# A spline convolution on one Trainium2 core: silu's products of two strips together on 64x32 tiles, and the first loads in another order

## The chip, the core and the metric

The kernel is one program on one core of a Trainium2 chip. The metric is the device time of one execution, in microseconds (us); less is better. The core has a matrix engine (TensorE, PE), three engines for elementwise work (VectorE or DVE, ScalarE or ACT, GpSimd or POOL), a queue that issues transfers (SyncE, SP), a memory of 128 partitions on the chip (SBUF) and banks for matmul results (PSUM). Each engine takes its instructions in the order in which they stand in the program and waits for others on semaphores.

## The reference

Four layers work on x of 8 images, 16 channels and 256 x 256 pixels, in float32. Each normalises its input by groups and adds its result to it: `x = x + layer(_gn(x), ...)`. Layer 0 is a convolution with routing, layer 2 attention over patches, layer 3 a convolution. The change is in layer 1, a 3x3 convolution in which every input value goes through silu and through eight cubic splines on a fixed grid, each with weights of its own:

```python
patches = _extract_patches(x, KSIZE, STRIDE, PAD)
grid = _grid()
bspl = _b_splines(patches, grid)
base_w = base_weight.sum(axis=2)
spl_w = (spline_weight * spline_scaler[..., None]).sum(axis=2)
out = jnp.einsum('bjhwn,ijn->bihw', jax.nn.silu(patches), base_w)
out = out + jnp.einsum('bjhwns,ijns->bihw', bspl, spl_w)
out = out + bias_weight[None, :, None, None]
```

## The kernel before

The layers follow one another in time: layer 0 up to about 4305 us of the profiled execution, layer 1 up to about 6135, then layers 2 and 3. `layer1` walks over 8 images of 16 strips, 128 strips in all, of 16 rows each. Even and odd rows are kept apart, so a strip is 8 pairs of rows.

*Bases.* `features` brings a strip in with a broadcast load of 1 MB (`xr`, L994): 16 channels, two rows of a pair and four grid offsets make the 128 partitions. In two halves of four pairs it makes two kinds of bases. ACT takes distances (L1012, L1015), DVE clips them twice (L1023, `a` and `e`), ACT squares both (L1029), DVE multiplies to cubes (L1032), POOL subtracts (L1041, the first kind, called total here), and DVE masks that into the second kind (L1044). At an image's ends DVE sets the rows outside (L1049). Three sets of bases (`ring`) stand in turn. DVE's L1023, L1044 and L1049 and POOL's L1041 are marked "shared" for the planner below.

*Silu.* `silus` loads a strip's raw rows twice, one row apart by two (`rs`, L1071), and the rows to be added to (`res`). ACT makes the silu (L1082) in four buffers `sring`, two for a strip.

*Products.* `conv_strip` sums a strip in one PSUM buffer `ps`, of which there are two. PE is used as four column tiles of 128 rows x 32 columns, one for each group of 32 output lanes: two output rows of 16 channels. Spline products are 12 groups of four matmuls: q = 0, 1 (the pair of rows and the one below it), two kinds, three columns dx. For the last output lanes q = 1 needs the first pair of the next strip's bases. Three groups of four matmuls with the silu weights `wm` follow. A float32 matmul shows as two records in the trace. All matmuls are recorded under L1106. Then DVE adds bias and `res` (`y`, L1143, two instructions), takes statistics (L1155), and SP stores the strip (L1158).

*Weights.* `prepare` loads spline weights `sw`, scalers `sc` and silu weights `main` (L933) into the places of bases that aren't in use yet. DVE multiplies the first two (L937), PE sums over the 9 inputs (L945 for splines, L970 for silu), DVE finishes `tw` (L954 to L966), ACT copies `wm` (L982).

*Order.* Nobody writes the order of the instructions by hand. Each step is given to `_Order` with its engine, a planned duration, what it reads and writes, and for a load a lag until its data is there. `_Order.run` plays the queues of all engines forward with these costs, up to four strips ahead, and of the steps that can start takes that with the earliest due time: the strip's number times `period`, less the planned length of what follows it. It adds 0.25 us when PE changes its `mode`. What stands in each engine's queue is the order in which it took the steps. `ahead` puts in other work: layer 2's weights are loaded at strip 2, the statistics of an image taken at its end (L1177).

*After it.* Layer 2 begins in `attend`: DVE normalises a patch into `t` (L1456), POOL adds embeddings (L1460), PE multiplies (L1466). `t` is taken from the pool `mid`.

Of the kernel before, what the change touches and what calls it, by code (L numbers as in the profile page):

```python
# [9 lines left out]
F32 = mybir.dt.float32  # L10
# [6 lines left out]
B, C, H, W = 8, 16, 256, 256  # L17
P = 128
# [13 lines left out]
def _consts():  # L32

    p = np.arange(P)
    hi, lo = p // 16, p % 16

    fold = np.stack([h * 16 + lo[:, None] == np.arange(32)[None, :] for h in range(2)], 1)
    unfold = np.zeros((4, 2, C, 2, 4, P), np.float32)
    for h in range(2):
        for k in range(4):  # L40
            unfold[k, h, :, h, k] = np.arange(C)[:, None] == lo[None, :]


    sel = np.stack([16 * g + 8 * h + hi[:, None] == np.arange(32)[None, :] for g in range(2) for h in range(2)], 1)
    spread = np.zeros((4, 2, 2, 8, 2, 2, 8, C), np.float32)
    for g in range(2):
        for h in range(2):
            for b in range(8):
                spread[:, g, h, b, g, h, b] = 1.0

    diff = np.zeros((B, C, C, B), np.float32)
    for i in range(C):
        for a in range(B - 1):
            diff[a, i, i, a] = 1.0
            diff[B - 1, i, i, a] = -1.0
        diff[:, i, i, B - 1] = 1.0 / B
    parts = {

        "pair": 0.5 * (p[:, None] // 2 == p[None, :] // 2),
        "diff": diff.reshape(P, P),  # L60

        "fold": fold.reshape(P, 2 * 32),
        "unfold": unfold.reshape(P, 8 * P),

        "sel": sel.reshape(P, 4 * 32),

        "spread": spread.reshape(P, 4 * P),
        "ident": np.eye(P),

        "group": (lo[:, None] // 2 == lo[None, :] // 2) / 16.0,  # L70

        "same_lo": lo[:, None] == lo[None, :],
        "ones": np.ones((P, P)),
        "mean": np.full((P, P), 1.0 / P),

        "same_c4": lo[:, None] == p[None, :] % 64 // 4,

        "hi8": hi[:, None] == np.arange(8)[None, :],
        "row0": p[:, None] == np.arange(16)[None, :],

        "middle": -(p[:, None] % 4 - 1.5),

        "pad": _padding(),

        "keep": np.stack([p >= 16, p < 112, p >= 64, p < 64], 1),

        "ident3": _ident3(),
    }
# [41 lines left out]
def _layout(w0, bw, sw, sc, bias, wq, bq, wk, bk, wv, bv, w3):  # L130
# [14 lines left out]
    sw = np.concatenate([sw, sw])  # L145
    sc = np.broadcast_to(sc.transpose(1, 2, 3, 0).reshape(1, C, 1, 81 * C), (2, C, 4, 81 * C)).reshape(P, 81 * C)
    bt = bw.transpose(1, 2, 3, 0).reshape(C, 9, 3, 3, C)
    main = np.zeros((8, C, 9, 3, 4, 2, C), np.float32)
    for ro in range(8):
        for dh in range(3):  # L150

            ri = ro + dh - 1 + (1 if ro < 6 else -1)
            main[ri, :, :, :, ro // 2, ro % 2] = bt[:, :, dh]
    main = main.reshape(P, 9 * 3 * P)
    b1 = np.tile(bias, 8).reshape(P, 1)

    qk = np.concatenate([wq.T, wk.T], 1).reshape(2, P, 512).transpose(1, 0, 2)
# [148 lines left out]
class _Net:  # L306
# [544 lines left out]
    def layer1(self, bc, bc4, images=range(B), strips=range(16)):  # L851
# [7 lines left out]
        with ExitStack() as st:  # L859
            one = st.enter_context(tc.tile_pool(name="l1_one", bufs=1))  # L860

            tw = one.tile([P, 2, 2, 3, 2, C], F32, name="tw")
            wm = one.tile([P, 3, 4, 2 * C], F32, name="wm")
            sbuf = st.enter_context(tc.tile_pool(name="l1_sb", bufs=1))
            psum = st.enter_context(tc.tile_pool(name="l1_ps", bufs=1, space=PSUM))
            b1 = one.tile([P, 1], F32, name="b1")
# [34 lines left out]

            places = dict(xr=3, d=3, a=3, e=3, res=4, rs=4, y=2)
            banks = dict(sq=3, ps=2)
            order = _Order({**places, **banks}, 13.3)

            def buf(kind, shape):
                n = {**places, **banks}[kind]
                pool = psum if kind in banks else sbuf
                return _Buf(kind, lambda: pool.tile(shape, F32, name=f"{kind}1", tag=kind, bufs=n))

            held = {}

            def edges(i, op):
                def pads():
# [9 lines left out]
            def prepare(op):  # L924

                at1, at2 = (ring[i].rearrange("p k m w -> p (k m w)") for i in (1, 2))
                sw, sc, main = at2[:, :2592], at2[:, 2592:3888], at1[:, :3456]
                ws = one.tile([P, 2, 3, 3, C], F32, name="ws")
                wf = ws.rearrange("p k h w o -> p (k h w o)")
                ps = buf("sq", [P, 1024])  # L930
                edges(0, op)
                for name, t in (("sw", sw), ("sc", sc), ("main", main), ("b1", b1)):
                    op("SP", 0.5, lambda name=name, t=t: nc.sync.dma_start(out=t, in_=self.d[name]), [], [(name,)], lag=16.0 if name == "main" else 10.0)  # L933

                def scaled():
                    for k in range(2):
# [31 lines left out]
                def sums_main():  # L968
                    for m in range(9):
                        nc.tensor.matmul(  # L970
                            ps()[:, 512:896],
                            self.k["ident"],
                            main[:, m * 384 : m * 384 + 384],
                            start=m == 0,
                            stop=m == 8,
                        )
# [1 line left out]
                op("DVE", 2.9, scaled, [("sw",), ("sc",)], [("sw",)], mode="shared")  # L978
                op("PE", 6.0, sums, [("sw",)], [(ps, 0), ("place", 2)])
                op("DVE", 3.5, finish, [(ps, 0)], [("tw",)], mode="shared")  # L980
                op("PE", 7.0, sums_main, [("main",)], [(ps, 1), ("place", 1)])
                op("ACT", 0.5, lambda: nc.scalar.copy(wm.rearrange("p d n m -> p (d n m)"), ps()[:, 512:896]), [(ps, 1)], [("wm",)])  # L982
                for i in (1, 2):
                    edges(i, op)

            def features(b, j, op):
# [12 lines left out]
                        .to_broadcast([2 * C, 4, pairs * W]),  # L999
                    )  # L1000

                op("SP", 0.5, fetch, [], [(xr, 0)], lag=6.0 if i else 13.0)
                for p in range(0, pairs, 4):
                    n = min(4, pairs - p)
                    us = 0.2 + 0.8 * n / 4
# [56 lines left out]

            def silus(b, j, op):

                i = b * 16 + j
                res = held[i] = buf("res", [P, 2, W])
                raw = [buf("rs", [P, 2, W]) for _ in range(2)]
                for r, to in ((1, res), (0, raw[0]), (2, raw[1])):

                    def fetch(r=r, to=to):  # L1070
                        nc.sync.dma_start(  # L1071
                            out=to().rearrange("p k w -> p (k w)"),
                            in_=self.x1[j, b, :, r : r + 8].rearrange("c r k w -> r c (k w)"),
                        )

                    op("SP", 0.5, fetch, [], [(to, 0)], lag=4.0 if i else 16.0)
                for n in range(2):
                    s = sring[i % 2 * 2 + n]
                    key = ("s", i % 2, n)
# [17 lines left out]

            def conv_strip(b, j, op):

                i = b * 16 + j  # L1100
                cur, res = ring[i % 3], held.pop(i)
                ps = buf("ps", [P, 2, W])

                def mm(n, k, lhs, rhs, start=False, stop=False):
                    out = ps()[32 * n : 32 * n + 32]
                    nc.tensor.matmul(  # L1106
                        out if k is None else out[:, k], lhs, rhs, start=start, stop=stop, skip_group_check=True
                    )

                for q in range(2):  # L1110
                    for kind in range(2):
                        for dx in range(3):

                            def products(q=q, kind=kind, dx=dx):
                                lhs = tw[:, kind, q, dx].rearrange("p r o -> p (r o)")
                                cols = slice(dx, dx + W)
                                both = cur[:, kind, 0:8].rearrange("p (k m) w -> p k m w", k=2)
                                for n in range(4):
                                    if n + q < 4:
                                        mm(n, None, lhs, both[:, :, n + q, cols], start=not (q or kind or dx))  # L1120
                                    else:
                                        mm(n, 0, lhs, cur[:, kind, 4, cols])
                                        last = cur[:, kind, 8] if j == 15 else ring[(i + 1) % 3][:, kind, 0]
                                        mm(n, 1, lhs, last[:, cols])
# [327 lines left out]

    def attend(self, mid, psum, b, c, pt, res, emb, wqk, wv, bqk, bv, bc, stats):
        nc = self.nc
        t = mid.tile([P, 2, 8, 32], F32, name="t")
        nc.vector.tensor_scalar(  # L1456
            t, pt[:, :, c], bc[:, 0, b, c : c + 1], bc[:, 1, b, c : c + 1], ALU.subtract, ALU.mult
        )
# [242 lines left out]
```

## Time and profile before

| what | us |
|---|---|
| median of 3 runs | 7646.63 |
| lowest and highest run | 7644.09, 7649.12 |
| the profiled execution | 7643.24 |
| its span, first to last instruction | 7641.5 |
| first load of layer 1, issued | 4305.97 |
| first product of layer 1, start | 4368.76 |
| last silu product of layer 1, start of the block | 6129.87 |
| first product of layer 2, start | 6140.35 |

The profile is one execution on the hardware. Its times are positions from the span's start. A line of a group or of a timeline names the code line (L1106), the engine, the operation and the data it wrote and read; xN is a number of records, and a bracket gives the idle time of the engine just before and what ended it. PE stands for matmuls and PEld for the loads of weights that go with them. PEclk is the share of full speed that TensorE's clock was granted.

### The profile page before, as it was taken

The numbers are of one execution on the slowest core, as the hardware profiler recorded it, in microseconds if no ns is written. First come the engines' busy times: TensorE is split into PE (matmuls) and PEld (weight loads), VectorE is DVE, ScalarE is ACT, GpSimd is POOL, SyncE is SP. The second block draws the span as 40 slices with busy tenths as digits, with TensorE's granted clock in tenths as the row PEclk, the third lists the DMA queues.
The fourth block names the chain that finished last, engine by engine and source line by source line (L and its number), as shares of the span: only waits on it lengthen the run. The fifth ranks groups of instructions, "written<-read, shape, count | busy, mean of one in ns | idle before, by whom it ended". The sixth has DMA issues, their size and how long they took to land.

```text
span 7641.5 us, 105946 instructions
## 1 busy us (share of the span) xinstructions
PE 6889.0 (90%) x43144; PEld 3276.6 (43%) x43144; DVE 5415.1 (71%) x6462; ACT 2691.9 (35%) x3835; POOL 3248.8 (43%) x1884
## 2 busy tenths in 40 slices
PE   4888888999898999998998499999999999999999
PEld 1333333333333333333333254554545566666634
DVE  5768888887888888888888688888888833333322
ACT  1222222222222222222222277777777712111200
POOL 0545555555555555555555444444444411111100
PEclk9999999999999999999999699999999999999999
DMA  6222222222222222222221344444445533333276
GB/s 243 67 65 76 77 77 77 77 77 77 77 77 77 77 77 77 77 77 76 77 76 50 105 153 156 153 152 152 154 151 161 159 114 97 86 85 97 68 214 189
DMA packets 451065, 813.01 MB, mean 106 GB/s; under 512 B 57490, under 2 KB 299282, under 8 KB 415250
## 3 DMA queue, kind: packets, MB, share of 16 engines
q1 hardware_dynamic: 380946, 738.85, 33.6%
q10 hardware_dynamic: 69632, 67.39, 3.0%
q8 instruction: 340, 5.57, 0.3%
q14 instruction: 147, 1.20, 0.1%
HBM read 595.63 MB, written 211.03 MB: 106 GB/s over the span
## 4 chain that ended last, share of the span: by engine, by line
PE 51%; POOL 21%; DVE 16%; issue 4%; ACT 3%; DMA 3%; SPq 0%; POOLq 0%; DVEq 0%; ACTq 0%
PE ps L1106 13%; POOL dd L765 11%; POOL s L765 8%; PE cv L545 8%; PE pqk L1466 6%; DVE dd L756 4%; PE p3s L1577 4%; PE cv L549 4%; PE pl L654 3%; PE po L1493 3%; PE pv L1473 3%; PE psc L1481 3%; PE fb L622 3%; DMA xr<-x1p 2%; POOL s L810 2%
## 5 line engine op out<-in xcount | busy, mean ns | idle before, releaser
L765 POOL TENSOR_TENSOR dd<-dd 128x1024 f32<-128x1024 f32 x512 | 1206.2, 2356 | 1594.9 <-DVE dd L756 1575.0
L1106 PE MATMUL ps<-bases,tw 128*32 128x512 f32 (+1 forms) x13824 | 1377.8, 550 | 109.6 <-DVE bases L1049 92.0
L756 DVE SCALAR_TENSOR_TENSOR dd<-rb,v 128x1024 f32<-128x1024 f32 (+1 forms) x1024 | 1075.2, 1082 | 206.7 <-PE rb L745 196.8
L554 ACT COPY v<-cv 128x1024 f32<-128x1024 f32 x512 | 518.2, 1012 | 1909.2 <-PE cv L549 1909.2
L1041 POOL TENSOR_TENSOR bases<-e,a 128x1024 f32<-128x1024 f32 (+1 forms) x264 | 744.9, 2823 | 1044.5 <-DVE e L1032 922.0
L545 PE MATMUL cv<-kt,w 128*128 128x512 f32 x2048 | 1090.9, 658 | 38.0 <-DVE dd L756 26.5
L1106 PEld LDWEIGHTS ps<-bases,tw 128*32 128x32 f32 x13824 | 732.4, 109 | 764.9 <-issue 458.3
L644 DVE TENSOR_TENSOR pr<-v,fb 128x2048 f32<-128x2048 f32 (+1 forms) x512 | 1019.5, 2014 | 24.9 <-PE pl L654 20.0
L745 PE MATMUL rb<-rs,ct_fold 32*128 32x512 f32 x3584 | 796.5, 658 | 8.3 <-ACT rs L727 2.7
L765 POOL TENSOR_TENSOR s<-s,dd 128x512 f32<-128x512 f32 x512 | 652.2, 1274 | 29.9
L545 PEld LDWEIGHTS cv<-kt,w 128*128 128x128 f32 x2048 | 366.1, 199 | 598.4 <-issue 389.7
L549 PE MATMUL cv<-kt,w 64*128 64x512 f32 x2048 | 590.9, 654 | 0.0
L654 PE MATMUL pl<-pr,ct_fold 128*32 128x512 f32 x3584 | 525.9, 610 | 61.0 <-DVE pr L644 60.3
L1460 POOL TENSOR_TENSOR t<-t,emb 128x512 f32<-128x512 f32 x128 | 162.1, 1266 | 961.9 <-DVE t L1456 950.8
L622 PEld LDWEIGHTS fb<-f,ct_fold 128*128 128x128 f32 x3072 | 376.7, 195 | 340.7 <-issue 296.7
L622 PE MATMUL fb<-f,ct_fold 128*128 128x128 f32 x3072 | 436.3, 290 | 90.7 <-DVE f L608 88.4
L1466 PE MATMUL pqk<-w_qk,t 128*128 128x512 f32 x1024 | 484.4, 596 | 7.6 <-POOL t L1460 7.6
L765 POOL TENSOR_TENSOR s<-v,dd 128x512 f32<-128x512 f32 x256 | 328.9, 1285 | 319.4 <-DVE dd L756 319.2
L1477 ACT ACTIVATE vt<-pv,w_b2v 128x128 f32<-128x128 f32 x512 | 146.0, 367 | 841.2 <-PE pv L1473 810.8
L1497 DVE TENSOR_TENSOR y<-po,res 128x512 f32<-128x512 f32 x128 | 88.5, 691 | 487.6 <-PE po L1493 487.6
L745 PEld LDWEIGHTS rb<-rs,ct_fold 32*128 32x128 f32 x3584 | 241.2, 188 | 380.7 <-DVE dd L756 211.7
L1032 DVE TENSOR_TENSOR e<-e,sq 128x1024 f32<-128x1024 f32 (+1 forms) x264 | 314.5, 1191 | 95.4 <-ACT sq L1029 95.4
(254 smaller groups left out, 8995.6 us busy)
## 6 DMA issues: line engine op xcount, KB each, us to landing
kt<-d SPq DMA_DIRECT2D x256, 516.0 KB
xr<-x1p SPq DMA_DIRECT2D x120, 1024.0 KB
rs<-x SPq DMA_DIRECT2D x256, 256.0 KB
d<-dn ACTq DMA_DIRECT2D x64, 516.0 KB
xs<-in_x_dram SPq DMA_DIRECT2D x16, 2048.0 KB
xs<-in_x_dram SPq DMA_DIRECT2D x64, 512.0 KB
res<-in_x_dram SPq DMA_DIRECT2D x64, 512.0 KB
x<-s SPq DMA_DIRECT2D x128, 256.0 KB
```

Source lines behind the costliest of these rows:

```text
L545: nc.tensor.matmul(ps()[:, n], w[:, 0, j, :], t[:, a : a + 2, 0:W], start=True, stop=False)
L549: nc.tensor.matmul(ps()[:, n], w[at, 1, j, :], t[at, a : a + 2, 2 - n : 2 - n + W], start=False, stop=True)
L554: nc.scalar.copy(v[h]()[:, 4 * g : 4 * g + 4, j * W : j * W + W], ps().rearrange("p n (a w) -> p (n a) w", w=W),)
L622: nc.tensor.matmul(fb()[:, k * P : k * P + P], unfold[:, h, k, :], f()[:, 3], start=True, stop=True)
L644: nc.vector.tensor_tensor(pr()[:, :n], v[h]()[:, 4 * g : 4 * g + n], p().unsqueeze(1).to_broadcast([P, n, 512]), ALU.mult,)
L654: nc.tensor.matmul(pl()[at : at + 32], sel[:, g, h, :], pr()[:, t, :], start=h == 0 and g == 0, stop=h == 1 and (g == 1 or t == 3),)
L745: nc.tensor.matmul(r()[:, n], spread[at, g, h, :], rs()[at], start=True, stop=True)
L756: nc.vector.scalar_tensor_tensor(dd()[:, :n], r()[:, :n], 1.0 / B, v[h]()[:, a : a + n], ALU.subtract, ALU.mult)
L765: op("POOL", us, lambda: nc.gpsimd.tensor_tensor(out[0](), a[0](), b[0](), ALU.add), a[1] + b[1], out[1])
L1041: nc.gpsimd.tensor_tensor(v, rows(part(e)), rows(part(a)), ALU.subtract)
L1106: nc.tensor.matmul(out if k is None else out[:, k], lhs, rhs, start=start, stop=stop, skip_group_check=True)
L1466: nc.tensor.matmul(ps, t[:, n, k * P : (k + 1) * P], wqk[:, n, :], start=n == 0, stop=n == 1)
```

## The change

Silu's weights: `main` was laid out for a matmul over eight input rows (128 partitions), with a different shift for each of the four groups of output rows. It is now laid out for four input rows (64 partitions), which holds for every group, twice over the partitions. It has 864 columns where it had 3456, and its sums and `wm` are as much narrower. DVE copies `wm`, where ACT did.

Silu's products: they are taken at the start of an odd strip's products, for that strip and the even one before it. A matmul now uses a tile of 64 rows x 32 columns; for each column group one matmul of the even and one of the odd strip stand on the two halves of the rows, and write two PSUM buffers. There are three groups of eight for a pair of strips, where each strip had three groups of four. The even strip is evicted after them. The odd strip's 12 groups of spline products come after them, and then its eviction.

Odd strips' raw rows: the two halves of the partitions are exchanged, so each of the two loads becomes two, of 64 partitions. `keep`, the mask of a row outside an image, follows that.

Ahead of the products: strip 0's `xr` is asked for before the weights, and the planned durations and lags of the first loads are set anew. Layer 2's weights are loaded at strip 6 in place of 2. The planner's `period` goes from 13.3 to 12.4, and the new silu group has the mode `r64`. In layer 2 `t` gets a pool of its own, allocated first.

```diff
-    main = np.zeros((8, C, 9, 3, 4, 2, C), np.float32)
-    for ro in range(8):
+    main = np.zeros((4, C, 9, 3, 2, C), np.float32)
+    for ro in range(2):
         for dh in range(3):
-
-            ri = ro + dh - 1 + (1 if ro < 6 else -1)
-            main[ri, :, :, :, ro // 2, ro % 2] = bt[:, :, dh]
-    main = main.reshape(P, 9 * 3 * P)
+            main[ro + dh, :, :, :, ro] = bt[:, :, dh]
+    main = np.tile(main.reshape(64, 9 * 96), (2, 1))
...
-            wm = one.tile([P, 3, 4, 2 * C], F32, name="wm")
+            wm = one.tile([P, 3, 2 * C], F32, name="wm")
...
-            order = _Order({**places, **banks}, 13.3)
+            order = _Order({**places, **banks}, 12.4)
...
-                sw, sc, main = at2[:, :2592], at2[:, 2592:3888], at1[:, :3456]
+                sw, sc, main = at2[:, :2592], at2[:, 2592:3888], at1[:, :864]
...
+                first = dict(sw=3.5, sc=1.8, main=1.2, b1=0.5)
                 for name, t in (("sw", sw), ("sc", sc), ("main", main), ("b1", b1)):
-                    op("SP", 0.5, lambda name=name, t=t: nc.sync.dma_start(out=t, in_=self.d[name]), [], [(name,)], lag=16.0 if name == "main" else 10.0)
+                    op("SP", first[name], lambda name=name, t=t: nc.sync.dma_start(out=t, in_=self.d[name]), [], [(name,)], lag=3.0)
...
-                            ps()[:, 512:896],
+                            ps()[:, 512:608],
                             self.k["ident"],
-                            main[:, m * 384 : m * 384 + 384],
+                            main[:, m * 96 : m * 96 + 96],
...
-                op("PE", 7.0, sums_main, [("main",)], [(ps, 1), ("place", 1)])
-                op("ACT", 0.5, lambda: nc.scalar.copy(wm.rearrange("p d n m -> p (d n m)"), ps()[:, 512:896]), [(ps, 1)], [("wm",)])
+                op("PE", 3.0, sums_main, [("main",)], [(ps, 1), ("place", 1)])
+                def finish_main():
+                    nc.vector.tensor_copy(wm.rearrange("p d m -> p (d m)"), ps()[:, 512:608])
+                op("DVE", 0.2, finish_main, [(ps, 1)], [("wm",)], mode="shared")
...
-                op("SP", 0.5, fetch, [], [(xr, 0)], lag=6.0 if i else 13.0)
+                op("SP", 0.5 if i > 2 else 2.8, fetch, [], [(xr, 0)], lag=6.0 if i else 8.0)
+                if not i:
+                    prepare(op)
...
-                        nc.sync.dma_start(
-                            out=to().rearrange("p k w -> p (k w)"),
-                            in_=self.x1[j, b, :, r : r + 8].rearrange("c r k w -> r c (k w)"),
-                        )
-                    op("SP", 0.5, fetch, [], [(to, 0)], lag=4.0 if i else 16.0)
+                        swap = i % 2 and r != 1
+                        for at, row, n in ((0, r + 4, 4), (64, r, 4)) if swap else ((0, r, 8),):
+                            nc.sync.dma_start(
+                                out=to()[at : at + 16 * n].rearrange("p k w -> p (k w)"),
+                                in_=self.x1[j, b, :, row : row + n].rearrange("c r k w -> r c (k w)"),
+                            )
+                    op("SP", 0.5 if i else 0.7, fetch, [], [(to, 0)], lag=4.0)
...
-                ps = buf("ps", [P, 2, W])
+                ps = open_ps[i] = buf("ps", [P, 2, W])
...
+                if i % 2:
+                    both = [(open_ps.pop(k), k) for k in (i - 1, i)]
+                    keys = [("s", k, n) for k in range(2) for n in range(2)]
+                    for dx in range(3):
+                        def silus(dx=dx):
+                            for n in range(4):
+                                for p, k in both:
+                                    half = n // 2 ^ k % 2
+                                    at = slice(64 * half, 64 * half + 64)
+                                    src = sring[k % 2 * 2 + n % 2]
+                                    mm(n, None, wm[at, dx], src[at, :, dx : dx + W], bool(k % 2 and not dx), dx == 2 and not k % 2, p)
+                        op("PE", 0.9, silus, [("wm",), *keys], [(p, 0) for p, _ in both], mode="r64")
+                    evict(b, j - 1, both[0][0], op)
...
-                for dx in range(3):
-                    def last(dx=dx):
-                        for n in range(4):
-                            src = sring[i % 2 * 2 + n // 3]
-                            mm(n, None, wm[:, dx, n], src[:, :, dx : dx + W], stop=dx == 2)
-                    op("PE", 0.86, last, [("wm",), ("s", i % 2, 0), ("s", i % 2, 1)], [(ps, 0)])
+                if i % 2:
+                    evict(b, j, ps, op)
+            def evict(b, j, ps, op):
+                res = held.pop(b * 16 + j)
                 y = buf("y", [P, 16, 2, 16])
...
-                if n == 2:
+                if n == 6:
                     for name, t in self.w2.items():
...
-                if not n:
-                    prepare(op)
                 if n < len(todo):
                     features(*todo[n], op)
...
+            self.tpool = st.enter_context(tc.tile_pool(name="l2_t", bufs=2))
...
-        t = mid.tile([P, 2, 8, 32], F32, name="t")
+        t = self.tpool.tile([P, 2, 8, 32], F32, name="t")
```

More of the change, by code (lines that the diff above doesn't have):

```diff
@@ L83, in _consts @@
         "pad": _padding(),
-        "keep": np.stack([p >= 16, p < 112, p >= 64, p < 64], 1),
+        "keep": np.stack([p >= 16, (p < 48) | (p >= 64), p >= 64, p < 64], 1),
         "ident3": _ident3(),
@@ L909, in buf @@
                 return _Buf(kind, lambda: pool.tile(shape, F32, name=f"{kind}1", tag=kind, bufs=n))
-            held = {}
+            held, open_ps = {}, {}
             def edges(i, op):
@@ L1100, in conv_strip, with mm @@
                 i = b * 16 + j
-                cur, res = ring[i % 3], held.pop(i)
-                ps = buf("ps", [P, 2, W])
-                def mm(n, k, lhs, rhs, start=False, stop=False):
+                cur = ring[i % 3]
+                ps = open_ps[i] = buf("ps", [P, 2, W])
+                def mm(n, k, lhs, rhs, start=False, stop=False, ps=ps):
                     out = ps()[32 * n : 32 * n + 32]
@@ L1117, in products @@
                                 both = cur[:, kind, 0:8].rearrange("p (k m) w -> p k m w", k=2)
+                                start = not (q or kind or dx or i % 2)
+                                stop = bool(i % 2 and q and kind and dx == 2)
                                 for n in range(4):
                                     if n + q < 4:
-                                        mm(n, None, lhs, both[:, :, n + q, cols], start=not (q or kind or dx))
+                                        mm(n, None, lhs, both[:, :, n + q, cols], start, stop)
                                     else:
-                                        mm(n, 0, lhs, cur[:, kind, 4, cols])
+                                        mm(n, 0, lhs, cur[:, kind, 4, cols], stop=stop)
                                         last = cur[:, kind, 8] if j == 15 else ring[(i + 1) % 3][:, kind, 0]
-                                        mm(n, 1, lhs, last[:, cols])
+                                        mm(n, 1, lhs, last[:, cols], stop=stop)
                             name = "vm"[kind]
```

## The prediction

> **What bounds the kernel now.** I read the shares of busy time first, then the costly groups, then layer 1 alone by stretches of time.
>
> ```profile
> PE 6889.0 (90%) x43144; PEld 3276.6 (43%) x43144; DVE 5415.1 (71%) x6462; ACT 2691.9 (35%) x3835; POOL 3248.8 (43%) x1884
> ...
> L1106 PE MATMUL ps<-bases,tw 128*32 128x512 f32 (+1 forms) x13824 | 1377.8, 550 | 109.6 <-DVE bases L1049 92.0
> ```
>
> ```profile
> 4368.70:6132.80 1764.10, 1677.94 (x16902) 885.59 (x16902) 1474.48 (x1749) 1262.77 (x1293) 734.57 (x260) 0.98 0.48 153
> ```
>
> Columns of the second: stretch, length, then busy time of PE, PEld, DVE, ACT, POOL, clock, DMA share, GB/s. Layer 1's products take 1764 us, PE is busy in 95% of it, and its idle time before the products is 110 us. So PE sets the pace within an image. DVE is the next engine, at 84%. The steady state shows in PE's timeline:
>
> ```profile
> 4706.59 2.79 PE L1106 MATMUL ps<-silu,wm 128*32 128x512 f32 x24
> 4709.16 10.55 PE L1106 MATMUL ps<-bases,tw 128*32 128x512 f32 x108
> 4719.47 2.82 PE L1106 MATMUL ps<-silu,wm 128*32 128x512 f32 x24
> ```
>
> From one silu block to the next is 12.88 us. A strip has 24 steps of four concurrent records for products and 6 for silu: 12.88/30 = 0.4295 us a step. A pair of strips takes 25.77 us. At an image's edge PE stops:
>
> ```profile
> 4589.94 10.54 PE L1106 MATMUL ps<-bases,tw 128*32 128x512 f32 x87 [9.65 <-DVE bases L1049]
> ```
>
> ```profile
> 4583.00:4593.00 10.00, 3.06 (x16) 0.90 (x20) 9.96 (x12) 4.39 (x5) 3.23 (x1) 0.51 0.63 183
> ```
>
> It waits 9.65 us for DVE, and its clock is halved into the restart. Per image before: 13 × 12.88 + 13.6 + 14.8 (two waits of about 1 and 2 us for DVE) + about 25 at the edge = 221, and 8 × 221 is the 1764 within 4. Ahead of the products:
>
> ```profile
> 4305.97 0.34 SPq L933 DMA_DIRECT2D bases<-in_main_dram  x1
> ...
> 4335.44 1.28 ACT L1082 ACT_TABLE_LOAD   x1 [29.76 <-DMA w_b2v<-in_b2v_dram]
> ...
> 4368.76 3.76 PE L1106 MATMUL ps<-bases,tw 128*32 128x512 f32 x20 [33.74 <-DVE bases L1049]
> ```
>
> ACT's first instruction is a silu whose rows are loaded late; everything behind it waits, and the first product starts 62.8 us after the first load. After the last product:
>
> ```profile
> 6138.18 1.00 DVE L1456 TENSOR_SCALAR t<-pt,g2a_bc 128x512 f32<-128x512 f32 x2 [3.03 <-issue]
> ```
>
> **What the Trainium skill says.** "TensorEngine Tiling (Array Packing)", Available Configurations, lists 64x32 as 8 independent tiles; Key Properties says that changing the mode drains TensorE. No 64x32 stands in this trace. Two row tiles do (64x128 in layer 0), concurrently; a change of mode costs 0.09 to 0.11 us there (2000.33 to 2007.3 us, the starts of L549 and L654 against their usual step). "TensorE: Matmul & The Clock Gate", Part 1, puts the clock at half after an idle window of about 3.4 us. The trace agrees so far: half clock after the 10 us gap (0.51 above), none after gaps of 2 us. "SBUF — State Buffer", Who interferes with whom, says that DVE and GpSimd lock one port pair for a whole instruction, and that issue order decides who waits. The trace agrees: L1041 on POOL takes 2.36 us alone and 3.27 when DVE's L1044 of 4710.15 started ahead of it.
>
> **The change, part by part.**
>
> *Silu on 64x32 tiles.* Per pair, 2 × 3 groups of four 128x32 matmuls (12 steps) become 3 groups of eight 64x32 (as many records, 6 steps). If eight tiles run in the time of four, PE saves 6 × 0.4295 = 2.58 us and pays two changes of mode, 0.22: 23.4 us of PE work a pair for 25.77. If eight cost like two fours, nothing is saved and 0.22 is lost. Each load of weights in the trace follows the last by 0.04 us, so eight take 0.32 of the 0.43 us step; I take full concurrency.
>
> *What the order makes of it.* PE's queue becomes: even strip's 12 groups, both silus, DVE evicts even; odd's 12 groups, DVE evicts odd; next even strip. Products with q = 1 of the even strip need row 0 of the strip after it. In the built order DVE makes those only behind the odd eviction, which itself waits for odd's last product. So a circle closes over each pair. I walk it with the trace's start-to-start times: DVE eviction 0.40, L1044 1.20, bn_stats 0.61, L1023 0.60, L1032 1.13; 0.17 from L1032's end to POOL, POOL 2.36, 0.03 on to PE or DVE. The rows are of this kind:
>
> ```profile
> 4714.91 0.68 DVE L1023 TENSOR_SCALAR a<-d 128x1024 f32<-128x1024 f32 x1
> 4715.51 0.69 DVE L1023 TENSOR_SCALAR e<-d 128x1024 f32<-128x1024 f32 x1
> ...
> 4716.71 1.21 DVE L1032 TENSOR_TENSOR a<-a,sq 128x1024 f32<-128x1024 f32 x1
> 4717.84 1.21 DVE L1032 TENSOR_TENSOR e<-e,sq 128x1024 f32<-128x1024 f32 x1
> ```
>
> From the end of odd's last product: 0.19 to the eviction; two of it, one L1044, bn_stats, three L1023 and one L1032 until POOL's first total starts, 5.79. Two more L1032 run beside that total and end 2.27 after its operand did; so the second total is ready 0.09 us before the first (2.36) is over, and POOL goes straight on. DVE's L1044, woken by the first total, comes 0.03 after its end and finds the port taken. Case A: two totals 4.60, L1044 1.28, 0.03: sum 11.9 until PE may start the last six steps of q = 1. Then 2.15 + 0.11 + 2.67 (six silu steps and their drain) + 0.11 + 10.34 (odd's 24 steps) = 15.4. The pair takes 27.27 us, of which PE is idle 3.3, in two pieces of 2.4 and 0.9; neither is long enough for the clock to fall. That is 1.5 us more than before in the steady stretch. What comes back is the edge: in the walk odd's 24 steps of an image's last strip keep PE running while DVE makes the next image's first bases, so an edge costs 3 us instead of 12 and leaves the clock alone. An image is 7 × 27.27 + 30.3 = 221.2, the same as before. Eight make 1770; I add 17 for the first two pairs (5) and for irregular places that a walk of the kernel before missed as well (some 12): 1787, or +23.
>
> *Odd strips' raw rows in swapped halves.* 128 more DMAs on SP's queue, 0.57 us to issue each, spread over 1764 us; SP is idle most of it and the transfer share is 0.48. Zero, covered by raw buffers two strips deep; without the cover half a microsecond a strip, 64 × 0.57 = 36.
>
> *Prologue.* The big broadcast goes first, then sw, sc; main is a quarter (432 KB for 1728), sums_main 96 wide for 384 (it took 5.97). ACT no longer starts with a silu. Walk: xr, sw and sc are some 3 MB, at the 410 GB/s of 4310 to 4320 us 7.5 us and 2 to land, so sc is there 9.6 after the first issue; L937 2.93; sums 7.23 behind it, 20; the weights' chain L954 to L966 took 5.5 (4353.59 to 4359.09), 26; beside it DVE and POOL make the first bases; L1044 and L1049 at the end, 29.7. Against 62.8: −33, and −25 to −38 if the loads land a few microseconds off. w2's loads, moved four strips later, leave SP's queue there; nobody needs them before layer 2.
>
> *wm copied by DVE instead of ACT, period 12.4, other lags.* 0.2 us once; the rest shows only in the order, which I walked.
>
> *t in its own pool.* DVE's 3.03 us wait ahead of layer 2 was for the last store, whose buffer t lay over. −3; zero if the loads issued at 6138.28 are then the late ones.
>
> Sum for A: −33 − 3 + 23 = −13. The profiled execution took 7643.24 (span 7641.5), 3.4 under the median 7646.63; A is 7630 against it and 7633 against the median. A measurement of this kernel tells about 0.2% (15.3 us) from no change.
>
> **The rivals.**
>
> B: DVE's L1044 gets the port between the two totals. It lacks 0.1 us: if a square on ACT or a cube is later by that, POOL's second total isn't ready. Then q = 1 runs on without its second wait; the walk gives 26.33 a pair, 216 an image, 1728 + 19 = 1747: −17. Sum −53: 7594. For it: the small margin. Against it: at 4575 us two totals stand back to back in the same pattern.
>
> C, slower: eight 64x32 matmuls don't fit a step. Place: the silu block, on the circle, so every 0.1 us of each step costs 6 × 0.1 × 64 = 38 us. It eats A's gain from 0.03 us a step (−13 + 13) and is slower by over 0.2% from 0.075. At 0.58 us a step (weight loads or PSUM in the way) it gives 7633 + 58 = 7691, with two fours 7633 + 165 = 7798. For it: the shape is nowhere in this trace, and the loads fill three quarters of a step. The skill's Gotcha 1 on that tiling page forbids two row tiles one PSUM bank at a time; the diff gives the halves different banks. Half clocks on each of 64 gaps would cost as much (1.8 each, 113).
>
> D: PE alone sets the pace, 23.4 a pair: 64 × 23.4 + 40 = 1538, −226 and −36: 7385. Against it: the circle stands in the built order. That the change does not do what it says is excluded by that order for the tiles; for the prologue it is the upper end of −25.
>
> **How the numbers follow.** A 0.45, B 0.25, C 0.25, D 0.05. Forecast: A's 7633; A's own range is 7615 to 7655 (prologue ±5 to 8, irregular places ±12). The range goes from under B to the middle price of C, 7585 to 7691; it leaves out D, C's upper half and a little of B. Faster by over 0.2% (under 7631): all of B and D, 0.13 of A: 0.43. Slower (over 7662): 0.23 of C and 0.05 of A: 0.28. Within: 0.29.
>
> **What would show it.** Silu blocks 26.3 (B) or 27.3 (A) apart for 2 × 12.88; a silu block's 48 records in 2.6 us (over 3.2: C); PE waiting about 2.4 us for POOL L1049 (the total's new line) and 0.9 for DVE once a pair; no 10 us wait at edges; the first product 30 us after the first load. A DVE that evicts odd strips without holding up the next bases would make all of A wrong.

## The result, and the profile after

| | before | after | foreseen |
|---|---|---|---|
| median of four runs | 7645.36 | 7689.09 | 7633 |
| ratio, 95% interval | | 1.0058, 1.0042 to 1.0074 | |
| span of the profiled execution | 7641.5 | 7693.0 | |
| start to the first load of layer 1 | 4306.0 | 4311.2 | 0 |
| first load to first product | 62.8 | 30.7 | −33 |
| first to last product of layer 1 | 1764.0 | 1850.5 | +23 |
| last product to the first of layer 2 | 7.6 | 4.4 | −3 |
| from there to the end | 1501.1 | 1496.2 | 0 |

The change made the kernel slower, by 44 us or 0.58%, where the forecast was no difference to speak of. The time lies at the upper end of the stated range. Three terms of the sum came as foreseen; the products of layer 1 cost 86.5 us more, not 23. The first and last rows (+5.3 and −4.9) are in code that the change leaves alone, but for t's pool. In the later kernels the first falls between 4303.8 and 4312.0 and the last between 1496 and 1500, so I take them as scatter between executions. The profiled execution, 7694.78 us, was the longest of the four.

The page after, first the shares of busy time and the group of the products, then the stretch of layer 1's products with the same columns as before:

```profile
PE 6831.9 (89%) x43144; PEld 3012.3 (39%) x43144; DVE 5508.7 (72%) x6463; ACT 2693.8 (35%) x3834; POOL 3119.0 (41%) x1884
...
L1119 PE MATMUL ps<-bases,tw 128*32 128x512 f32 (+1 forms) x13824 | 1444.0, 560 | 223.1 <-POOL bases L1049 181.7
```

```profile
4341.90:6192.40 1850.50, 1624.09 (x16902) 619.80 (x16902) 1574.10 (x1758) 1271.43 (x1300) 611.63 (x262) 0.97 0.50 147
```

PE has 54 us less to do in layer 1 (1624 for 1678), yet the stretch is longer: PE is busy in 88% of it where it was in 95%. Its idle time before products doubled to 223 us, and what ends it is now mostly POOL's total (L1049) instead of DVE's edge rows. PE no longer sets the pace.

PE's timeline over one pair in the middle of an image, as foreseen for case A:

```profile
4651.11 2.81 PE L1119 MATMUL ps<-silu,wm 64*32 64x512 f32 x48
4653.85 16.73 PE L1119 MATMUL ps<-bases,tw 128*32 128x512 f32 x164
4672.64 2.78 PE L1119 MATMUL ps<-bases,tw 128*32 128x256 f32 x30 [2.07 <-POOL bases L1049]
4676.06 2.35 PE L1119 MATMUL ps<-bases,tw 128*32 128x256 f32 x22 [0.64 <-DVE bases L1052]
4678.34 1.95 PE L1119 MATMUL ps<-silu,wm 64*32 64x512 f32 x32
```

From silu block to silu block is 27.23 us; the walk said 27.27. The block's 48 records are over 2.74 us after its start, changes of mode included: eight 64x32 tiles do run in the time of four. The two waits of the prediction are there, 2.07 and 0.64 us. But of the 63 distances between pairs only 15 look like this. A pair later in an image:

```profile
5194.02 2.81 PE L1119 MATMUL ps<-silu,wm 64*32 64x512 f32 x48
5196.75 6.21 PE L1119 MATMUL ps<-bases,tw 128*32 128x512 f32 x56
5203.45 4.94 PE L1119 MATMUL ps<-bases,tw 128*32 128x256 f32 x52 [0.48 <-POOL bases L1049]
5211.37 6.21 PE L1119 MATMUL ps<-bases,tw 128*32 128x512 f32 x56 [2.98 <-POOL bases L1049]
5218.77 2.78 PE L1119 MATMUL ps<-bases,tw 128*32 128x256 f32 x30 [1.20 <-POOL bases L1049]
5222.19 2.35 PE L1119 MATMUL ps<-bases,tw 128*32 128x256 f32 x22 [0.63 <-DVE bases L1052]
5224.47 1.95 PE L1119 MATMUL ps<-silu,wm 64*32 64x512 f32 x32
```

It takes 30.45 us, with two more waits for POOL, 0.48 and 2.98 us. The median of the 63 is 28.6. POOL is only the last link. ACT's timeline in the same stretch, and what SP issued ahead of it:

```profile
5195.12 1.24 ACT L1020 ACTIVATE d<-xr,bd,sd 128x1024 f32<-128x1024 f32 x1 [6.44 <-DMA xr<-x1p]
...
5225.79 1.24 ACT L1020 ACTIVATE d<-xr,bd,sd 128x1024 f32<-128x1024 f32 x1 [6.66 <-DMA xr<-x1p]
```

```profile
5205.69 2.39 SPq L1083 DMA_DIRECT2D rs<-x  x4
5210.73 0.62 SPq L1185 DMA_DIRECT2D x<-y  x1
5211.40 0.58 SPq L1083 DMA_DIRECT2D res<-x  x1
5212.66 12.44 SPq L1000 DMA_DIRECT2D xr<-x1p  x2
```

The strip's broadcast load xr is issued at 5212.66, when its buffer comes free, and ACT gets it at 5225.79, 13.1 us later; ACT has waited 6.66 us, and DVE, POOL and PE stand behind ACT. (The 12.44 us are those of two loads; the second waits for its buffer.) Ahead of xr on SP's queue are the four half loads of raw rows that the change made out of two. Over layer 1, ACT waits 210 us for xr; before it was 69.

At both ends the profile after reads as the prediction had it: the first product 30.7 us after the first load, and no wait ahead of `t`, against the 3.03 us of before.

```profile
4341.92 3.64 PE L1119 MATMUL ps<-bases,tw 128*32 128x512 f32 x16 [10.77 <-DVE bases L1057]
...
6194.70 0.94 DVE L1482 TENSOR_SCALAR t<-pt,g2a_bc 128x512 f32<-128x512 f32 x2
```

### The profile page after: what moved, and what is told of

Its sections match the earlier page's. It is cut to its first block, busy times and chain, and to the rows that moved or that the text cites. A ratio compares the mean times of both kernels' runs of the same rounds, so it can differ in the third digit from the quotient of the medians.

```text
span 7693.0 us, 106047 instructions
## 1 busy us (share of the span) xinstructions
PE 6831.9 (89%) x43144; PEld 3012.3 (39%) x43144; DVE 5508.7 (72%) x6463; ACT 2693.8 (35%) x3834; POOL 3119.0 (41%) x1884
## 3 DMA queue, kind: packets, MB, share of 16 engines
q1 hardware_dynamic: 380946, 737.52, 34.2%
## 4 chain that ended last, share of the span: by engine, by line
PE 46%; POOL 23%; DVE 19%; DMA 6%; issue 4%; ACT 2%; SPq 0%; POOLq 0%; DVEq 0%; ACTq 0%
POOL dd L764 11%; PE cv L544 8%; POOL s L764 8%; PE ps L1119 8%; PE pqk L1492 6%; DMA xr<-x1p 4%; PE p3s L1603 4%; DVE dd L755 4%; PE cv L548 4%; PE pl L653 3%; PE po L1519 3%; POOL bases L1049 3%; PE pv L1499 3%; PE psc L1507 3%; PE fb L621 3%
## 5 line engine op out<-in xcount | busy, mean ns | idle before, releaser
L1119 PE MATMUL ps<-bases,tw 128*32 128x512 f32 (+1 forms) x13824 | 1444.0, 560 | 223.1 <-POOL bases L1049 181.7
L544 PE MATMUL cv<-kt,w 128*128 128x512 f32 x2048 | 1094.8, 660 | 39.3 <-DVE dd L755 26.5
L1049 POOL TENSOR_TENSOR bases<-e,a 128x1024 f32<-128x1024 f32 (+1 forms) x264 | 616.4, 2345 | 1246.2 <-DVE e L1040 1180.4
L1119 PEld LDWEIGHTS ps<-bases,tw 128*32 128x32 f32 x13824 | 567.2, 111 | 1120.4 <-issue 537.3
L1052 DVE SCALAR_TENSOR_TENSOR bases<-xr,xm,bases 128x1024 f32<-128x1024 f32 (+1 forms) x264 | 455.1, 1726 | 95.2 <-POOL bases L1049 95.1
L1040 DVE TENSOR_TENSOR a<-a,sq 128x1024 f32<-128x1024 f32 (+1 forms) x264 | 315.0, 1193 | 111.2 <-ACT sq L1037 111.0
```

Source lines behind the costliest of these rows:

```text
L544: nc.tensor.matmul(ps()[:, n], w[:, 0, j, :], t[:, a : a + 2, 0:W], start=True, stop=False)
L1049: nc.gpsimd.tensor_tensor(v, rows(part(e)), rows(part(a)), ALU.subtract)
L1119: nc.tensor.matmul(out if k is None else out[:, k], lhs, rhs, start=start, stop=stop, skip_group_check=True)
```

## The experiments

The traces leave three theories. Theory 1: the circle of the prediction is right, 27.2 us a pair, and on top of it odd strips' xr lands late, behind a bunch of row loads. Theory 2: the order on the engines alone stretches the pairs. Theory 3: the half loads of 64 partitions are slow themselves. All times are medians; each was run beside the kernel before, which stayed at 7642.7 to 7643.4. Brackets give the ratio to it and its 95% interval. A pair is timed from the start of one silu block to the next, 63 times in a run.

**Order of the first loads alone (e1).** In the kernel before, with the new planned times and lags of the first loads and layer 2's weights at strip 6:

```diff
-                op("SP", 0.5, fetch, [], [(xr, 0)], lag=6.0 if i else 13.0)
+                op("SP", 0.5 if i > 2 else 2.8, fetch, [], [(xr, 0)], lag=6.0 if i else 8.0)
+                if not i:
+                    prepare(op)
...
-                if not n:
-                    prepare(op)
```

> The kernel before with the change's order of first loads alone: xr of strip 0 ahead of the weights, the new planned times and lags, layer 2's weights at strip 6; silu products and weights stay as they were. Theory 1 (the prologue is worth what the changed kernel's trace shows, a first product 32 us earlier, and is lost again in the pairs): first product 20 to 33 us earlier than before, less than the whole because main keeps its 1728 KB; steady strips stay at 12.88; about 7618 us. Rival (the reordering disturbs the strips that follow): no gain, 7640 to 7660.

7617 us (0.996, 0.9945 to 0.9975). The first product starts 38.1 us after the first load (62.8 before, 30.7 with the quarter-sized main), and the products take 1766.9 us for 1764.0. So the gain of the prologue is real and stands by itself; the changed kernel has it and loses it later.

**One raw load a strip (e2).** The changed kernel, both silus from the rows of the first; the rows of the second load are left out:

```diff
-                raw = [buf("rs", [P, 2, W]) for _ in range(2)]
-                for r, to in ((1, res), (0, raw[0]), (2, raw[1])):
+                raw = [buf("rs", [P, 2, W])] * 2
+                for r, to in ((1, res), (0, raw[0])):
```

> The changed kernel with one raw load a strip in place of two: both silus read the rows of the first (it leaves out the shifted rows of the second, and the order of the compute instructions stays). 512 KB of 4 MB a pair and 3 of 13 transfers go. Theory 1 (pairs stretch from 27.2 to 28.5-30.6 us because the odd strip's xr, issued right behind a bunch of raw rows, lands 8 to 13 us after issue in place of 5): ACT's wait for xr falls from 210 to under 80 us, most pairs are 27.2, about 7640 us. Theory 2 (the pairs stretch by the order on DVE, POOL and ACT alone): 7689, within 8 us.

7661 us (1.0022, 1.0015 to 1.0029): 28 of the 49 us that theory 1 wanted, and outside theory 2. ACT still waits 191 us, over twice what I expected. With half of the raw bytes gone xr still lands 10.1 us after issue in the median. Bytes in a bunch are not the whole of it.

**Odd rows whole (e3).** The changed kernel without the exchange of halves, so odd strips' silu products take other rows:

```diff
-                        swap = i % 2 and r != 1
+                        swap = False
```

> The changed kernel with odd strips' raw rows in one transfer of 128 partitions in place of two of 64 (the halves are not exchanged, so the odd strips' silu products take other rows); as many bytes, 128 transfers fewer. Theory 1 (bytes in a bunch): within 10 us of 7689. Theory 3 (transfers of 64 partitions are themselves slow, or 128 more issues hold SP up): ACT's wait for xr falls by more than half, about 7640 us.

7631 us (0.9984, 0.9976 to 0.9993). Theory 3's figure, not theory 1's: as many bytes as in the changed kernel, but 58 us less. 38 of 63 pairs take 27.2 to 27.3, ACT waits 97 us for xr, and the products take 1787.4 us, which is the 1787 of the prediction's case A. The pair after the longer one shown above takes 27.24 us here, for 30.64 in the changed kernel:

```profile
5184.59 2.81 PE L1119 MATMUL ps<-silu,wm 64*32 64x512 f32 x48
5187.33 16.63 PE L1119 MATMUL ps<-bases,tw 128*32 128x512 f32 x164
5206.12 2.78 PE L1119 MATMUL ps<-bases,tw 128*32 128x256 f32 x30 [2.17 <-POOL bases L1049]
5209.55 2.35 PE L1119 MATMUL ps<-bases,tw 128*32 128x256 f32 x22 [0.65 <-DVE bases L1052]
5211.83 1.05 PE L1119 MATMUL ps<-silu,wm 64*32 64x512 f32 x6
```

**Four xr buffers (e4).** The changed kernel; d has two buffers and the ninth pair is loaded by itself, to make room:

```diff
-            places = dict(xr=3, d=3, a=3, e=3, res=4, rs=4, y=2)
+            places = dict(x9=1, xr=4, d=2, a=3, e=3, res=4, rs=4, y=2)
```

> The changed kernel with four xr buffers in place of three; to make room, d has two buffers for three and the ninth pair of an image's last strip is loaded by itself. A load can be issued a strip earlier. Theory 1: the wait of ACT for xr goes nearly to zero, pairs are 27.2 to 27.3 throughout (28.5 at the second of an image), layer 1's products take about 1790 us for 1850, 7630 us. Theory 2: 7689; if two d buffers hinder ACT, more.

7629 us (0.998, 0.9972 to 0.9989), products 1787.8 us. ACT never waits for xr, though the half loads are still there. So the way by which they hurt is xr alone: given a strip's lead, they cost nothing that shows. Theory 2 is out.

**POOL made to let DVE go first (e5).** e4, with a copy of one column on POOL ahead of a strip's second total:

```diff
+                        if p == 4:
+                            nc.gpsimd.tensor_copy(look, t[:, 1, 0, 1:2])
                         nc.gpsimd.tensor_tensor(v, rows(part(e)), rows(part(a)), ALU.subtract)
```

> e4 (four xr buffers) with one more instruction on POOL ahead of the second total of a strip: a copy of one column (128x1) that DVE's masking of the first half has written. POOL must then let DVE's masking go first, which is rival B of the prediction made to happen. Theory 1 (in the changed kernel POOL's second total takes the port and DVE's masking waits a whole total for it): pairs go from 27.2 to 26.3 (second of an image 27.6 for 28.5), less some 0.1 for the copy; layer 1's products 30 us shorter than in e4, about 7600 us. Rival (who goes first doesn't matter, the sum of the two engines' work does): within 8 us of e4's 7629.

7609 us (0.9955, 0.994 to 0.997), 20 less than e4, for an expected 30. DVE's masking in the changed kernel, then POOL's two totals of that moment, then both at the same place in e5:

```profile
4672.62 3.38 DVE L1052 SCALAR_TENSOR_TENSOR bases<-xr,xm,bases 128x1024 f32<-128x1024 f32 x1 [0.31 <-POOL bases L1049]
```

```profile
4670.22 4.70 POOL L1049 TENSOR_TENSOR bases<-e,a 128x1024 f32<-128x1024 f32 x2 [5.92 <-DVE e L1040]
```

```profile
4672.80 1.29 DVE L1059 SCALAR_TENSOR_TENSOR bases<-xr,xm,bases 128x1024 f32<-128x1024 f32 x1 [0.29 <-POOL bases L1056]
```

```profile
4670.39 2.37 POOL L1056 TENSOR_TENSOR bases<-e,a 128x1024 f32<-128x1024 f32 x1 [5.19 <-DVE e L1045]
4674.15 0.58 POOL L1055 COPY look<-bases 128x1 f32<-128x1 f32 x1 [1.39 <-DVE bases L1059]
```

In the changed kernel POOL runs its two totals back to back and DVE's instruction takes 3.38 us. In e5 POOL waits, DVE's takes 1.29, and pairs go from 27.2 to 26.4 (48 of 63 between 26.3 and 26.5); the walk of rival B said 26.33. More than the missing 10 us went at images' edges, where a pair now takes 34.6 to 37.1 us for 30.2 to 33.5 in e4: the seven edges take 34 us more, the other 56 pairs 56 less. Why the edges grow the runs don't show.

**Odd eviction later (e6).** The changed kernel; an odd strip's eviction is handed to the planner with the next strip's work:

```diff
                 if i % 2:
-                    evict(b, j, ps, op)
+                    waiting.append((b, j, ps))
+                if waiting and (not i % 2 or j == 15):
+                    evict(*waiting.pop(), op)
```

> The changed kernel with the eviction of an odd strip given to the planner with the following strip's work, 12.4 us later in due time (in an image's last strip as before); transfers as in the changed kernel. Theory 1 (the pair's length is the circle over DVE: bases for the next strip stand behind the odd eviction, which waits for the odd products): the circle is broken, pairs go to 24.3 by my walk with the trace's durations where transfers allow; those that wait for xr stay longer; between 7480 and 7570 us. Rival (DVE's and POOL's sum of work or PE sets the pair's length): within 20 us of 7689.

7547 us (0.987, 0.9854 to 0.9887), 142 less than the changed kernel. 40 of 63 pairs run from 24.3 to 26.3 us, held up by xr (ACT waits 213 us for it).

**Late eviction and four xr buffers (e7).**

> e6 with e4's four xr buffers (d two, ninth pair by itself). Theory 1: both causes gone, pairs of 24.3 nearly throughout (walk: 1626 us from first to last product, plus some 15), 7629 - 149 = 7480, with 7470 to 7510 as bounds. Rival (with shorter pairs the transfers can't keep up, 4 MB in 24.3 us): 7520 to 7560, ACT waiting for xr or silu waiting for rows.

With e4's buffers added: 7475 us (0.9779, 0.9764 to 0.9793), products 1629.7 us. 40 of 63 pairs lie between 24.2 and 24.5. One of them:

```profile
4904.77 2.81 PE L1123 MATMUL ps<-silu,wm 64*32 64x512 f32 x48
4907.51 21.59 PE L1123 MATMUL ps<-bases,tw 128*32 128x512 f32 x216
4929.03 1.05 PE L1123 MATMUL ps<-silu,wm 64*32 64x512 f32 x6
```

In these 24.26 us no wait is long enough for the timeline to show it, and PE is busy for 24.12. Against e4, with the same buffers and pairs of 27.2, only the moment at which the planner gets the odd evictions is new. So the circle did set the pair's length. With the circle gone PE is nearly always busy, except in the first pairs and at the edges of images, which still take 26.6 to 34.2 us.

**Halves exchanged by ACT (e8).** The changed kernel with rows loaded whole, and silu of odd strips in two instructions that write to the other 64 partitions:

> The changed kernel with odd strips' raw rows loaded whole, and their halves exchanged by ACT: silu of an odd strip in two instructions of 64 partitions that write to the other half, each as long as one of 128 (1.5 us for 0.8 a silu, 1.5 us of ACT a pair). Theory 3 (transfers of 64 partitions slow the xr behind them): as the kernel with whole rows, 7631, within 10 us. Rival (ACT has no time for it): 7660 or more, pairs over 28 us with DVE waiting for squares.

7632 us (0.9985, 0.9979 to 0.9992): as e3, with the exchange that e3 leaves out. Each instruction on 64 partitions takes 0.81 us, where one on 128 takes 0.80, so ACT has some 100 us more to do; it had the time.

**Halves in the kernel before (e9).** The reverse test, odd strips' raw rows in two transfers there:

```diff
+                        split = i % 2 and r != 1
+                        for at, row, n in ((0, r, 4), (64, r + 4, 4)) if split else ((0, r, 8),):
```

> The kernel before with odd strips' raw rows in two transfers of 64 partitions each, not exchanged: 128 transfers more, nothing else. There the order on SP is xr first and the rows after it, strip by strip. Theory 1 + 3 (64-partition transfers are slow on a few engines and hurt what is issued right behind them): xr leads, so little is lost; 7640 to 7660 us. Rival (128 more issues, or half transfers wherever they stand, cost by themselves): 7675 to 7700, as in the changed kernel.

7665 us (1.0027, 1.0017 to 1.0038), a little above what I gave theory 1 + 3 and below the rival. ACT's wait for xr goes from 69 to 105 us. In the profiled execution the products take 20 us longer, and 4.5 more pass between the first load and the first product. xr mostly leads the rows there, but not in every strip, and where it doesn't the loss is the same in kind. I had taken the order to be the same in all strips.

**All rows in halves (e10).** The changed kernel; the loads that were whole are split too:

```diff
-                        for at, row, n in ((0, r + 4, 4), (64, r, 4)) if swap else ((0, r, 8),):
+                        for at, row, n in ((0, r + 4, 4), (64, r, 4)) if swap else ((0, r, 4), (64, r + 4, 4)):
```

> The changed kernel with every row load in two transfers of 64 partitions, not only the odd strips' raw rows: 12 halves a pair in place of 4, same bytes and same results. Theory 3 (halves run on the same four of the engines, so 256 KB take twice as long, and xr, which uses all, waits for those four): each whole that is split adds some 1.3 us ahead of xr, three to four of them a pair, so the odd xr lands 16 to 20 us after issue and pairs grow to 31 to 35 us; 7800 to 8000 us. Rival (halves are spread over all engines; the cost is in the number of transfers): 7690 to 7730.

7913 us (1.035, 1.0333 to 1.0367), pairs of 32.8 in the median; ACT waits 477 us for xr. The rival is far off. My landing time of 16 to 20 us for the odd xr was too long: its median is 13.0. When the parts of a transfer are done can be read from its completion marks, the steps by which it raises its semaphore, each with its time in the trace. For one odd xr of each kernel, in us after its issue (sixteen marks each; the xr of 5200.17, 5212.66 and 5065.15 us):

```
odd rows whole (e3)      8 at 6.3 to 7.1,  8 at 7.2 to 8.1
changed kernel           8 at 7.6 to 8.0,  4 at 9.0 to 9.4,  4 at 11.0 to 13.1
all rows in halves (e10) 12 at 6.2 to 6.9, 4 at 12.6 to 13.4
```

An xr with nothing ahead of it has all sixteen between 4.7 and 5.4. A row load of 128 partitions leaves eight marks when it lands, a half leaves four (both also leave one about 1 us after the issue). In e10, where all row loads are halves, the late group of an odd xr is four of its sixteen in 61 of 64 strips. So a half seems to run on four of the transfer engines, and all halves on the same four: were they spread, more of xr's marks would be late. The trace doesn't name the engines. By this count, and as an estimate, 256 KB in two halves keep those four busy twice as long as a whole would. I found the rule afterwards in the Trainium skill, "DMA: Bandwidth & Descriptors", section "Why a DMA increments its semaphore by 16 and not by 1": the number of engines is the largest k ≤ 16 that divides the outermost dimension of both sides, and they are the lowest-numbered. A row load's outermost dimension is 8 rows, a half's is 4. The marks agree, 8 and 4; that the engines are the lowest-numbered no run here shows.

**Channels outermost (e11).** If that is it, halves can be had for nothing: put the 16 channels ahead of the rows.

```diff
-                                in_=self.x1[j, b, :, row : row + n].rearrange("c r k w -> r c (k w)"),
+                                    in_=self.x1[j, b, :, row : row + 4].rearrange("c r k w -> c r (k w)"),
```

> The changed kernel with the silu operands' partitions in another order, channel before row within each half, so that the raw rows' transfers have 16 channels as their outermost dimension where they had 8 or 4 rows; weights, mask, bias and scale follow, the results are the same. All raw rows, even strips' too, are now halves of 64 partitions: 8 of them a pair in place of 4. Theory 3 in its sharper form (a transfer is spread over as many engines as its outermost dimension allows: 8 for rows whole, 4 for halves, 16 here): the odd xr lands 8 us after issue or earlier, pairs are 27.2, 7620 to 7635 us. Rival (64 partitions, or the number of transfers, are what is slow): 7690 to 7720, more than the changed kernel since more are halved.

7631 us (0.9985, 0.9979 to 0.9992), products 1787.8 us, with eight half loads a pair. Each leaves sixteen marks, and an odd xr (that of 5169.59 us) has its own at 6.7 to 8.6. Neither the number of transfers nor the 64 partitions was at fault, but the outermost dimension.

**Channels outermost and late eviction (e12).**

> e11 with e6's late eviction and three xr buffers. Theory: with the transfers spread, xr is in time without a fourth buffer, pairs of 24.3 as in e7, 7475 to 7500 us. Rival (at 24.3 us a pair three xr buffers are too few whatever the transfers): 7510 to 7550, as e6.

7475 us (0.978, 0.9764 to 0.9797), with three xr buffers and 34 us of waiting for xr. This and e7 are the best versions, 2.2% under the kernel before.

## Why the prediction was wrong

*The sum.* −33, −3 and +23 were foreseen; −32.1, −3.2 and +86.5 came.

*The step that failed* is "Odd strips' raw rows in swapped halves", put at "Zero, covered by raw buffers two strips deep". I counted its 128 issues against SP's free time and its bytes against a transfer share of 0.48, and looked for the consumer of these rows, silu, which indeed waits for them only once in the changed kernel, 2.7 us. Who stands behind them in the transfer engines I did not ask: xr, whose buffer has come free late and whose lead is short. And the zero takes a half to be half the work of a whole, where by its marks it has as much to move on each of half as many engines. The measured price is 58 us (changed kernel to e3, e8 or e11), more than the 36 I gave for a lost cover (which counts one of the two further issues of an odd strip; both make 73). The share of 0.48 is a mean over sixteen engines, while the late marks of xr are those of four.

*The circle* was right in place, in order and in size: 27.2 for 27.27 where xr is in time, 26.4 for rival B's 26.33, 24.3 when it is broken. PE's two waits were 2.07 and 0.64 us in the changed kernel, for 2.4 and 0.9. One of its terms is written short: with the 0.17 us from the cube to POOL the 5.79 become 5.96, and only so do the terms make the 11.9. With whole rows the kernel's time is 7631, 2 under A's 7633. That POOL going first is what lengthens DVE's masking is shown by e5; how small the margin is, 0.1 us in the prediction, no run varied.

*The irregular places,* +17, hold as a sum: 1787.4 and 1787.8 measured in e3 and e4. Where they lie was not compared one by one.

*C*, the slower rival, named the wrong place. Its price, 7691, lies beside the result by accident: the silu block takes 2.74 us, and e3 removes the loss without touching it. The loads of weights that C counts were misread: in the trace of before the four of a step start within 0.05 us, then 0.38 pass; 0.04 is only the longest of their three distances. *D* is out for the change as built, because of the circle. With the circle broken (e7) most pairs come near it, 24.26 us for its 23.4; by the starts of the matmuls, 0.8 us of that lies in two short stops. First pairs and edges of images keep the whole kernel at 7475, above D's 7385.

*The prologue and t's pool:* −32.1 and −3.2 in the trace. Of the prologue, e1 shows 25 as the order's alone; the other 7 go with the smaller main, which was not tried by itself, nor was t's pool.

*The range* held the time for a cause that was not in it, which was luck; the chance of 0.28 for slower was given to C, but for 0.05 of A.

## What to carry to other kernels

Before a transfer is split, look at the outermost dimension of what remains and at what is issued right behind it, not at the free time of its queue or at the mean share of the engines. When a step is moved behind a long wait on an in-order engine, follow the queue until it comes back to the same step: that sum is the new period, and a step with slack of its own, like the odd eviction here, should stand late in it. A gain that is measured early in a program (32 us) can be spent later without a trace at the place where it arose: lay the stages side by side.

## What the runs showed of the hardware that was not expected

- A row load of 128 partitions with 8 rows outermost leaves 8 completion marks, one of 64 partitions with 4 rows outermost 4, with 16 channels outermost 16; behind halves alone 12 of xr's marks come at 6.2 to 6.9 us and four at 12.6 to 13.4, as if all halves kept to the same four engines.
- With nothing ahead of it the 1 MB broadcast lands 5.3 us after its issue; behind four such halves it took up to 13.1 (10.9 in the median of odd strips).
- ACT wrote silu of partitions 0 to 63 to 64 to 127 and back, at no cost that shows in the kernel's time (7632 for 7631); two instructions of 0.81 us took the place of one of 0.80.
- Eight float32 matmuls on 64x32 tiles, writing two buffers, take the time of four on 128x32: 48 records in 2.74 us with both changes of mode.
